# Two GNN layers over 32 batches: the last batch turned back to natural row order and stored by SyncE, two loads moved ahead, another order of the last additions

## The chip, the cores and the metric

The kernel runs on one core of one Trainium2 chip. The metric is the device time of one execution in microseconds; of several executions the median counts. In the profile PE is TensorE, PEld its weight loads, DVE VectorE, ACT ScalarE, POOL GpSimd and SP SyncE; a `q` behind a name means that engine's sequencer (waits, branches, DMA issues).

## The reference, cut to what matters

```python
# x: 32 x 512 x 512, adj: 512 x 512
h = relu(layernorm(x))                       # layer 0
x = x + einsum('nm,bmd->bnd', adj, h) @ W0 + b0
h = relu(layernorm(x))                       # layer 1: attention, 8 heads
q, k, v = h @ Wq + bq, h @ Wk + bk, h @ Wv + bv
scores = q k^T / 8 + (1 - adj) * -1e9        # per head
x = x + softmax(scores) v @ Wo + bo
```

The mask of layer 1 is so steep that each row's softmax has all its weight on the one column where adj is largest. The kernel tests this on the device at the start; it then computes layer 1 of row n as `h[argmax of adj in row n] @ (Wv Wo)` plus a constant row. Only the rows of h that some argmax names are needed, at most 336 of 512.

## The kernel before, in words

A batch is a 512 x 512 matrix of 1 MB, held as four chunks of 128 rows (chunk c is `X[b][:, c, :]`). From batch 5 on (`FIRST` is 4), the loop runs with the rows of a batch in another order, chosen so that much of `adj` is zero and layer 0 needs fewer products ("sparse", `spread`). `plan.xi` lists which natural row lies at which place: chunks are gathered from DRAM by it (`load_x`) and scattered back by it (`store_rows`, line 516, an indirect DMA on GpSimd). Where `back(b)` holds, a batch is first scattered into a DRAM buffer `xn` in natural order (`turn_back`, line 468), loaded again (`come_back`, line 478, four plain loads on SyncE), and then stored with plain DMAs (line 510). Before the change this is so for batches 29 and 30.

Iteration b of the loop has 21 steps. Each is a list of small pieces put there by `put(batch, step, f)`; a step's pieces are emitted just before the instruction that takes one result of TensorE out of PSUM. Steps 0 to 6 lie in layer 0 of batch b, 7 to 13 in the aggregation of batch b+1, 14 to 20 in layer 1 of batch b-1. So every engine's queue is in an order written out by hand, and an engine that waits holds up all that is behind it. `behind` makes each indirect DMA also wait for the PSUM result taken last before it in that order (`tick`), so that GpSimd keeps step with the rest.

The end is special. In iteration 31 (the last batch), steps 7 to 13 lie in layer 1 of batch 29 (TensorE from 968.87 us) and steps 14 to 20 in that of batch 30 (from 976.85 us). Layer 1 gives only the needed rows, z; they go to DRAM (`put_z`, line 773) and are fetched to the rows that want them (`fetch`, line 784, four gathers: `sel` for batch 29, `yT` for batch 30) and added (`add_z`, line 787), after which the chunk is stored. Layer 1 of batch 31 takes another way, to have no such round trip behind it: its h is stored as it is (`put_h`, line 683, two DMAs on SyncE), all 512 rows that the argmaxes name are gathered (`get_all`, line 495, four gathers `h<-hs`), and `layer1_rows` transposes chunk r (line 715), copies it (ScalarE, 716), multiplies it by `wvo` (727), adds it to x (730) and stores it, chunk by chunk. The additions and stores of batches 29 and 30 are placed between these chunks. Iteration 32 is only a list of pieces ahead of `layer1_rows`: the last z stores of batch 30, the transposes of chunk 0, `add_cvo` (719, a constant row added to x) and, before the change, `come_back(30)`.

`get_all` reads h by `plan.pq` (for rows in the loop's order); `plan.pi` is the same list for rows in natural order.

Behind the last instruction of this path stands a branch over the other path (line 980), and then the closing block (line 1658): SyncE waits for the semaphores of all DMAs, each engine reports (`DRAIN`), GpSimd collects the reports.

Of the kernel before, what the change touches and what calls it, by code (L numbers as in the profile page):

```python
# [408 lines left out]
def single_path(ctx: ExitStack, tc: tile.TileContext, x, adj, out, kept, room):  # L409
    nc = tc.nc  # L410
    B, N, D = x.shape
    C, DC = N // P, D // P
# [25 lines left out]
    hs_d = [dram.tile([N, D], F32, name=f"hs{i}") for i in range(3)]  # L438
# [5 lines left out]
    plan = Plan(tc, consts, dram, adj, kept, upper, B) if folded else None  # L444
# [5 lines left out]
    def phase(batches, sparse):  # L450
        with ExitStack() as inner:
            small = inner.enter_context(tc.tile_pool(name="small", bufs=4))
            ps_m = inner.enter_context(tc.tile_pool(name="ps_m", bufs=6, space=PSUM))
            ps_t = inner.enter_context(tc.tile_pool(name="ps_t", bufs=2, space=PSUM))
            run_phase(batches, sparse, small, ps_m, ps_t)

    def run_phase(batches, sparse, small, ps_m, ps_t):
        ordered = folded and (sparse or batches[0] == 0)

        def natural(b):  # L460
            return not ordered or b <= FIRST

        def back(b):
            return sparse and ordered and B - 3 <= b < B - 1

        def turn_back(b, chunks):
            for c in chunks:
# [20 lines left out]
        def behind(move):  # L488
            for taken in clock:
                tc.add_manual_dep(move.ins, taken.ins.name, mybir.DependencyInfo(  # L490
                    mybir.DependencyClass.Sync, mybir.DependencyReason.DATA), reason="in step")
            return move

        def gather(dst, rows, at, **more):
            return behind(nc.gpsimd.indirect_dma_start(out=dst, out_offset=None, in_=rows,  # L495
                                                       in_offset=bass.IndirectOffsetOnAxis(ap=at, axis=0), **more))
# [11 lines left out]
        def store_rows(b, c, eng):  # L508
            if natural(b) or back(b):
                stored = eng.dma_start(out[b, c * P:(c + 1) * P, :], X[b][:, c, :])  # L510
                if sparse:
                    for other_rows in stored_rows:
                        tc.declare_no_dep(stored.ins, other_rows.ins, reason="other rows")
                    direct_rows.append(stored)
                return
            stored = behind(nc.gpsimd.indirect_dma_start(  # L516
                out=out_rows, out_offset=bass.IndirectOffsetOnAxis(ap=plan.xi[:, b, c:c + 1], axis=0),
                in_=X[b][:, c, :], in_offset=None))
            nc.gpsimd.memset(gap, 0.0)
            for other_rows in stored_rows + direct_rows:  # L520
                tc.declare_no_dep(stored.ins, other_rows.ins, reason="other rows")
            stored_rows.append(stored)
# [87 lines left out]
        def places():  # L610
            table = dram.tile([N, 1], I32, name="table", bufs=1)
            nc.sync.dma_start(table.rearrange("(c p) o -> c (p o)", p=P), dest_r)
            return table

        def look_up(table, chunks):
            for c in chunks:
                gather(place[:, c:c + 1], table, idx[:, c, 0:1])
# [89 lines left out]

        def get_all(b, chunks=range(C)):
            for c in chunks:
                gather(hs[0][:, c, :], hs_d[b % 3], idx[:, c, 0:1] if natural(b) else plan.pq[:, c:c + 1])  # L710

        def transpose_all(r):
            pt = ps_t.tile([P, DC, P], F32, name="pt")
            for d in range(DC):
                nc.tensor.transpose(pt[:, d, :], hs[0][:, r, d * P:(d + 1) * P], ident)
            nc.scalar.copy(hs[1][:, :, r * P:(r + 1) * P], pt)
# [4 lines left out]
        def layer1_rows(b):  # L721
            for r in range(C):
                bank = ps_m.tile([P, D], F32, name="mm")
                for d in range(DC):
                    if d == 2 and r + 1 < C:
                        transpose_all(r + 1)
                    nc.tensor.matmul(bank, hs[1][:, d, r * P:(r + 1) * P], wvo[:, d, :], start=(d == 0),  # L727
                                     stop=(d == DC - 1))
                x_r = X[b][:, r, :].rearrange("p (q c e) -> p q c e", q=4, c=4)
                nc.vector.tensor_add(x_r, bank.rearrange("p (c q e) -> p q c e", q=4, c=4), x_r)  # L730
                store_rows(b, r, nc.sync)
                if sparse and r == 0:
                    for c in range(C):
                        add_z(B - 3, c, nc.sync)
                    fetch(B - 2)
                if sparse and r >= 2:
                    for c in ((0, 1, 2), (3,))[r - 2]:
                        add_z(B - 2, c, nc.scalar if c % 2 else nc.sync)
                for i in range(0 if sparse else 2):
                    add_z(B - 3 + r // 2, 2 * (r % 2) + i, nc.sync if r < 2 else nc.scalar)  # L740
# [34 lines left out]
        def place_of(b, c):  # L775
            return (place if natural(b) else plan.home if back(b) else plan.place)[:, c:c + 1]
# [5 lines left out]
        def fetch(b, chunks=range(C)):  # L782
            for c in chunks:
                gather(late_z[b][:, c, :], z_d[b % 3], place_of(b, c))

        def add_z(b, c, eng):
            nc.vector.tensor_add(X[b][:, c, :], late_z[b][:, c, :], X[b][:, c, :])
            store_rows(b, c, eng)
# [18 lines left out]
        for b in batches:  # L807
            todo = [[] for _ in range(21)]

            def put(batch, step, f, *args):  # L810
                if 0 <= batch < B:
                    todo[step].append(lambda: f(batch, *args))
# [78 lines left out]
            if b < B - 1:  # L891
                put(b, 20 if not several else 17, get_h)
            elif not sparse:
                put(b, 13, get_all)
                for c in range(C):
                    put(b, 15 + c, add_cvo, c)
            elif b == B - 1:
                for c in range(C):
                    put(b, 13, get_all, [c])
                    put(b - 1, 2 * c, turn_back, [c])  # L900
            if sparse and b == B - 2:
                for c in range(C):
                    put(b - 1, c, turn_back, [c])
                put(b - 1, 9, come_back)
# [37 lines left out]
            if sparse and b == B:  # L942
                put(b - 1, 1, lambda b: transpose_all(0))
                put(b - 2, 2, put_z, 6, S, range(2, 4))
                put(b - 2, 2, put_z, 0, 6, range(2, 4))
                put(b - 2, 2, come_back)
                for c in range(C):
                    put(b - 1, 1, add_cvo, c)
            if b == 1:
                tables = []  # L950
                put(1, 0, lambda b: tables.append(places()))
                for c in range(C):
                    put(1, 3 + c, lambda b, c: look_up(tables[0], [c]), c)
# [15 lines left out]
        if batches[-1] == B:  # L969
            layer1_rows(B - 1)  # L970
# [692 lines left out]
```

## Time and profile before

| | us |
|---|---|
| median of 3 runs (1020.17 to 1023.55) | 1021.16 |
| the profiled execution | 1016.16 |
| its span, first to last instruction | 1014.4 |
| PE busy | 988.0 (97%) |
| DVE busy | 801.9 (79%) |
| POOL busy | 591.1 (58%) |
| ACT busy | 586.1 (58%) |
| last TensorE matmul ends | 1001.57 |
| last engine instruction ends (POOL, line 519) | 1004.68 |

The profiled execution lies 5.0 us under the median of the runs, and 1.76 us of it lie outside its span. Sums below are made on the clock of the profile, in us from the start of the span. TensorE's granted clock is 0.992 of full over the span and 1.00 in the last 30 us until the matmuls end. Where a row of the timeline stands for several instructions, its second number is from the start of the first to the end of the last.

### The profile page before, as it was taken

How to read it: one execution, taken by the hardware profiler on the slowest of the kernel's cores; microseconds unless marked ns; L12 is line 12 of the kernel's file. 1: busy time of each engine (PE TensorE's matmuls, PEld its weight loads, DVE VectorE, ACT ScalarE, POOL GpSimd, SP SyncE). 2: the span in 40 equal slices, each digit the busy share in tenths (PEclk: the TensorE clock that was granted, in tenths of full speed). 3: DMA queues.
4: the chain of work that ended last, by engine and by line, in shares of the span. 5: the costliest groups of instructions: out<-in, count | busy, mean ns of one | idle time of the engine just before them, and what ended most of it. 6: DMA issues, size and time to landing. Idle time of an engine off the chain costs nothing.

```text
span 1014.4 us, 17265 instructions
## 1 busy us (share of the span) xinstructions
PE 988.0 (97%) x5627; PEld 886.9 (87%) x5627; DVE 801.9 (79%) x1792; ACT 586.1 (58%) x1282; POOL 591.1 (58%) x666
## 2 busy tenths in 40 slices
PE   7999999998999999999999999999999999999994
PEld 6468999897999999999999999999999999999882
DVE  4998897667888877778887777788877777888773
ACT  2765364556755555667655555676555556675330
POOL 1032366656666666666666666666766666667543
PEclk8999999999999999999999999999999999999998
DMA  9214558788888888888888888998888888888867
GB/s 312 82 65 152 113 164 250 220 223 219 207 226 206 201 221 209 231 221 207 211 194 207 219 207 227 225 223 202 201 203 213 209 219 227 221 209 207 210 209 265
DMA packets 161884, 208.90 MB, mean 206 GB/s; under 512 B 16556, under 2 KB 104376, under 8 KB 161784
## 3 DMA queue, kind: packets, MB, share of 16 engines
q0 software_dynamic: 44544, 120.10, 48.5%
q1 hardware_dynamic: 115480, 85.66, 29.2%
q10 hardware_dynamic: 1760, 1.93, 0.5%
q8 instruction: 46, 0.75, 0.3%
q14 instruction: 54, 0.44, 0.2%
HBM read 123.55 MB, written 84.09 MB: 205 GB/s over the span
## 4 chain that ended last, share of the span: by engine, by line
PE 72%; DMA 2%; POOL 2%; issue 2%; DVE 1%; ACT 1%; SPq 0%; POOLq 0%; ACTq 0%; DVEq 0%
PE mm L532 50%; PE mm L652 13%; PE mm L655 7%; PE mm L649 2%; DMA hc<-hs 1%; POOL x L495 1%; DMA pi<-posd,idx 1%; DMA z<-zr 1%; DMA hs<-h,dest 0%; POOL hs L692 0%; POOL out_dram L516 0%; POOL yT L495 0%; PE mm L727 0%; ACT h L379 0%; DVE st L361 0%
## 5 line engine op out<-in xcount | busy, mean ns | idle before, releaser
L588 DVE TENSOR_TENSOR x<-mm,x 128x512 f32<-128x512 f32 x217 | 148.8, 686 | 130.2 <-PE mm L532 128.2
L495 POOL DMA_INDIRECT x<-z,pplace x96 | 153.5, 1599 | 81.8 <-ACT yT L660 40.9
L379 ACT ACTIVATE h<-x,off,rstd 128x512 f32<-128x512 f32 x256 | 196.1, 804 | 7.3 <-DVE off L370 4.0
L532 PE MATMUL mm<-w_t,sel 128*128 128x256 f32 x744 | 171.7, 380 | 1.3 <-DVE x L588 1.3
L365 ACT ACTIVATE rstd<-mv,eps 128x2 f32<-128x2 f32 (+1 forms) x90 | 26.3, 292 | 241.8 <-DVE mv L362 241.8
L532 PEld LDWEIGHTS mm<-w_t,sel 128*128 128x128 f32 x744 | 140.6, 190 | 21.4 <-DVE x L588 2.5
L361 DVE BATCH_NORM_STATS2 st<-x 128x6 f32<-128x512 f32 x234 | 157.7, 674 | 1.1
L652 PE MATMUL mm<-ap,h 128*128 128x256 f32 x648 | 157.8, 380 | 0.0
L516 POOL DMA_INDIRECT out_dram<-x,xi x100 | 124.8, 1248 | 42.5 <-DVE zs L578 21.0
L495 POOL DMA_INDIRECT x<-in_x_dram,xi x108 | 104.0, 963 | 72.5 <-DVE x L588 37.4
L652 PEld LDWEIGHTS mm<-ap,h 128*128 128x128 f32 x648 | 114.9, 191 | 11.1
L495 POOL DMA_INDIRECT at<-in_x_dram,gi x81 | 76.9, 949 | 72.8 <-DVE st L361 25.0
L532 PE MATMUL mm<-w_s,yT 128*128 128x256 f32 x496 | 117.3, 379 | 0.8 <-ACT zs L580 0.8
L532 PE MATMUL mm<-hTs,wvo_t 128*128 128x168 f32 x720 | 113.4, 307 | 2.4 <-ACT zs L580 1.4
L532 PEld LDWEIGHTS mm<-hTs,wvo_t 128*128 128x128 f32 x720 | 105.4, 190 | 3.1 <-ACT zs L580 1.9
L580 ACT ACTIVATE zs<-mm,cvo_c 128x168 f32<-128x168 f32 x240 | 83.0, 398 | 38.2 <-PE mm L532 37.8
L532 PEld LDWEIGHTS mm<-w_s,yT 128*128 128x128 f32 x496 | 92.8, 190 | 12.3 <-ACT zs L580 1.0
L655 PEld LDWEIGHTS mm<-ag,adjT 128*128 128x128 f32 x648 | 89.3, 191 | 5.6
L655 PE MATMUL mm<-ag,adjT 128*128 128x128 f32 x648 | 89.7, 275 | 0.0
L627 DVE TENSOR_TENSOR x<-x,b_r 128x512 f32<-128x512 f32 x124 | 84.0, 678 | 0.0
L660 ACT COPY yT<-mm 128x512 f32<-128x512 f32 x108 | 61.5, 571 | 29.6 <-PE mm L655 29.6
L532 PE MATMUL mm<-hT,wvo 128*128 128x168 f32 x480 | 78.3, 306 | 0.0
(323 smaller groups left out, 1678.7 us busy)
## 6 DMA issues: line engine op xcount, KB each, us to landing
hc<-hs SPq DMA_DIRECT2D x124, 176.0 KB
z<-zr SPq DMA_DIRECT2D x120, 96.0 KB
hs<-h SPq DMA_DIRECT2D x52, 192.0 KB
z<-zr SPq DMA_DIRECT2D x120, 80.0 KB
hs<-h SPq DMA_DIRECT2D x52, 160.0 KB
out_dram<-x SPq DMA_DIRECT2D x26, 256.0 KB
x<-in_x_dram SPq DMA_DIRECT2D x12, 256.0 KB
x<-xn SPq DMA_DIRECT2D x8, 256.0 KB
```

Source lines behind the costliest of these rows:

```text
L361: self.nc.vector.bn_stats(st, self.src[:, self.chunks[i], :])
L365: self.nc.scalar.activation(self.rstd[:, 0:len(self.chunks)], self.mv[:, :, 1], AF.Sqrt, bias=self.eps)
L379: self.nc.scalar.activation(dst, src, AF.Relu, bias=self.off[:, i:i + 1], scale=self.rstd[:, i:i + 1])
L495: return behind(nc.gpsimd.indirect_dma_start(out=dst, out_offset=None, in_=rows, in_offset=bass.IndirectOffsetOnAxis(ap=at, axis=0), **more))
L516: stored = behind(nc.gpsimd.indirect_dma_start(out=out_rows, out_offset=bass.IndirectOffsetOnAxis(ap=plan.xi[:, b, c:c + 1], axis=0), in_= ...
L532: nc.tensor.matmul(bank[:, m, 0:half], lhs[:, k, m * P:(m + 1) * P], rhs[:, k, :], start=(first and m == 0 and k == 0), stop=(k == 1), ski ...
L580: taken = nc.scalar.activation(dst[:, m, :], bank[:, m, :], AF.Identity, bias=cvo_c[:, 2 * i + m:2 * i + m + 1])
L588: return nc.vector.tensor_add(dst, bank, dst)
L627: nc.vector.tensor_add(X[b][:, c, :], X[b][:, c, :], b0_r)
L652: nc.tensor.matmul(two(bank, j), H0[b][:, j, cols], two(plan.ap[:, j, :], j), start=False, stop=False, skip_group_check=True)
L655: nc.tensor.matmul(bank[:, j * P:(j + 1) * P], extra[:, j - 1, cols], plan.ag[:, j - 1, j * P:(j + 1) * P], start=False, stop=(j == C - 1) ...
L660: tick(nc.scalar.copy(yT[:, d, :], bank))
```

## The change

Batch 31 is turned back too: `back(b)` now holds for it. Its four chunks are scattered to `xn` at steps 7 to 10 of iteration 31, and loaded back at step 15. Its h is then gathered by `plan.pi`, its rows are added in natural order, and SyncE stores them with line 510 in place of GpSimd's line 516. `come_back(30)` moves from iteration 32 (behind the z stores) to step 9 of iteration 31, which on SyncE's queue is ahead of `put_h(31)`. `fetch(30)` moves from inside `layer1_rows` (behind the store of chunk 0) to the list ahead of it. VectorE's order in `layer1_rows` was: chunk 0, batch 29's four, chunk 1, chunk 2, batch 30's chunks 0, 1, 2, chunk 3, batch 30's chunk 3. It is now: chunk 0, batch 29's four, chunk 1, batch 30's chunk 0, chunk 2, batch 30's chunks 1, 2, 3, chunk 3.

```diff
         def back(b):
-            return sparse and ordered and B - 3 <= b < B - 1
+            return sparse and ordered and B - 3 <= b
...
-                gather(hs[0][:, c, :], hs_d[b % 3], idx[:, c, 0:1] if natural(b) else plan.pq[:, c:c + 1])
+                gather(hs[0][:, c, :], hs_d[b % 3], idx[:, c, 0:1] if natural(b) else plan.pi[:, c:c + 1])
...
                 if sparse and r == 0:
                     for c in range(C):
                         add_z(B - 3, c, nc.sync)
-                    fetch(B - 2)
-                if sparse and r >= 2:
-                    for c in ((0, 1, 2), (3,))[r - 2]:
+                if sparse and 0 < r < C - 1:
+                    for c in ((0,), (1, 2, 3))[r - 1]:
                         add_z(B - 2, c, nc.scalar if c % 2 else nc.sync)
...
                 for c in range(C):
                     put(b, 13, get_all, [c])
                     put(b - 1, 2 * c, turn_back, [c])
+                    put(b, 7 + c, turn_back, [c])
+                if sparse:
+                    put(b - 1, 9, come_back)
+                    put(b, 15, come_back)
...
                 put(b - 1, 1, lambda b: transpose_all(0))
                 put(b - 2, 2, put_z, 6, S, range(2, 4))
                 put(b - 2, 2, put_z, 0, 6, range(2, 4))
-                put(b - 2, 2, come_back)
                 for c in range(C):
                     put(b - 1, 1, add_cvo, c)
+                put(b - 2, 3, fetch)
```

## The prediction, on record before the changed kernel ran

> **What bounds the kernel now.** First the chain that ended last: up to 986 us it is nearly all TensorE, back to back, so nothing is won there; past it come GpSimd, waits and transfers. The change touches the trace from 963 us on, so I read that end by stage. Columns: stretch, its length, busy us of PE, PEld, DVE, ACT, POOL with counts, granted clock, busy share of the DMA engines, GB/s.
>
> ```profile
> 971.00:975.00 4.00, 4.00 (x31) 4.00 (x30) 3.52 (x12) 3.30 (x8) 0.00 (x0) 1.00 0.02 4
> 975.00:979.00 4.00, 4.00 (x31) 4.00 (x30) 3.86 (x8) 2.47 (x6) 0.00 (x0) 1.00 0.76 281
> 985.00:990.00 5.00, 4.18 (x16) 2.21 (x15) 4.13 (x6) 1.75 (x4) 3.29 (x5) 1.00 0.85 241
> 990.00:996.00 6.00, 6.00 (x19) 2.80 (x18) 2.67 (x4) 0.59 (x1) 3.96 (x6) 1.00 1.03 312
> 996.00:1002.00 6.00, 5.57 (x16) 2.35 (x14) 3.37 (x5) 0.59 (x1) 3.82 (x6) 1.00 1.05 412
> 1002.00:1006.50 4.50, 0.00 (x0) 0.00 (x0) 1.98 (x3) 0.00 (x0) 1.07 (x2) 0.78 1.06 400
> ```
>
> The DMA engines are empty from 971 to 975 and full from 990 to 1006.5, with 400 GB/s until 5 us after the last matmul. GpSimd has its hole in the same place. The timeline of GpSimd and VectorE (start, duration, engine, line; in brackets the idle time ahead):
>
> ```profile
> 969.30 0.17 POOL L762 MEMSET zs<- 128x64 f32 x1
> 980.10 1.00 POOL L495 DMA_INDIRECT h<-hs,pq  x1 [10.63 <-DVE adjT_s L347]
> ...
> 1002.64 0.68 DVE L730 TENSOR_TENSOR x<-mm,x 128x512 f32<-128x512 f32 x1
> 1003.61 0.96 POOL L516 DMA_INDIRECT out_dram<-x,xi  x1 [2.99 <-DVE x L730]
> 1003.91 0.69 DVE L787 TENSOR_TENSOR x<-yT,x 128x512 f32<-128x512 f32 x1 [0.58 <-DMA yT<-z,phome]
> 1004.57 0.11 POOL L519 MEMSET gap<- 128x1 f32 x1
> ```
>
> TensorE ends at 1001.57, but chunk 3 of batch 31 is added 1.07 us later, because batch 30's additions ahead of it wait for their gathers, whose transfers queue. Each DMA of this stretch lands 4.6 to 7.6 us after its issue, where z stores from 977.7 to 980.6 took 1.8 to 2.1 (landings are the trace's semaphore records). The last store is issued at 1004.63 and lands at 1009.21.
>
> Then the close, line 1658 (min/median/max in ns, first and last start):
>
> ```profile
> L1658 POOLq DRAIN  x3: 51/103/4592, 1008.7 to 1014.1; - x3
> ```
>
> GpSimd's first DRAIN runs from 1008.67 to 1013.26, and the other engines have reported by 1010.13 (SyncE, last). From 1013.26 to the end is 1.12. So 3.1 us of the end are GpSimd's alone.
>
> **The change, part by part.**
>
> *turn_back(31).* Four scatters on GpSimd. Its neighbours in the trace (L468) take 0.96 plus a memset of 0.11 and start every 1.28. x of batch 31 is complete at 970.38 (last L588), so they run from about 970.7 to 975.7. The hole is 10.6 us long, and the next GpSimd instruction starts at 980.1: nothing on GpSimd. If the hole were gone, they would cost 5.1 us.
>
> *come_back(30), moved.* Four loads on SyncE, 0.43 each (median of L478). They wait for the scatters of batch 30, the last of which landed at 971.01; so they are issued from 971.1 to 972.9. Behind them on SyncE is `put_h(31)`, ready at 974.70: 1.8 us of slack. In the tail the same 1.05 MB goes away (it was issued at 988.80 to 991.81): at 412 GB/s 2.5 us of a full queue.
>
> *come_back(31).* Four loads on SyncE behind the z stores of batch 29 (issued until 981.66), so 981.7 to 983.5; next on SyncE are z stores at 985.94. They need the turned rows, landed by about 978. Their user, `add_cvo`, ran at 986.70 to 989.20 and must only be done by 990.43. ScalarE's four z stores reuse the DMA semaphores of these loads, so they may wait until they land, near 987, up to 1 us later than before; behind them on ScalarE is the copy of chunk 1, 1.7 us later. I take nothing, at most 1 us.
>
> *The price: h of batch 31 comes later.* Between 972 and 979 the DMA engines moved 1.05 MB (h, landed 979.24). Now 3.15 MB want to pass there: the load of x30 and the scatters of batch 31, 2.1 MB, ahead of or beside h. The gap from 971.9 to 975.5 holds some 3.6 us of work: by the 383 GB/s that h itself reached at its best (977 to 978), 3.15 MB take 8.2 us and end at 980.1, which lands near 980.5; so h is 1.3 us late. With the rate of the same load of batch 29 alone (1.05 MB from 946 to 949.8, 275 GB/s) it would be 4.5 us late; with a perfect fit 0. The Trainium skill ("DMA: Bandwidth & Descriptors", Queues, rings and completion order) says that a DMA engine takes packets round-robin from the queues that have work: GpSimd's scatters then take half while h goes out, which speaks against the change. The same page (Specifications) puts the limit of HBM per core at 358 GB/s; by it they take 8.8 us and h is 1.9 us late. The rows above show 400 to 412 over 10 us in this traffic, above the rule, so I stay with 1.3.
>
> The first h gather then starts at 981.4. Chunk 0 landed 4.0 us after its issue (984.11), 0.6 us before TensorE wanted it (984.69). Beside the loads of x31 I add 0.4: 985.8, so TensorE stands still for 1.1 us (0 to 2.5 with the bounds 0 and 2.7 for h; 6 at the worst rate). Chunks 1 to 3 had 2.3, 5.6 and 7.6 us of slack. TensorE ends at 1002.7. GpSimd's zero fill of z (L762, behind the gathers) and the z transposes and stores of batch 30 shift by the same 1.3.
>
> *fetch(30) and the stores of batch 31.* The gathers `yT` lay behind one L516 (0.99 + 0.12) and began at 993.21, when the z stores, landed by 992.33, had let them. Now they follow the `sel` gathers at once: shifted by 1.3, z lands about 992, since 1 MB less runs beside it, so the gathers start at 992.4 to 996.2. Their time to land was 6.3 to 6.9; with x30's 1.05 MB gone (2.5 us of queue) I take 5, so the last is there at 1001.2 (4 to 6.9: 1000.2 to 1003.1). VectorE's last `add_z` of batch 30 ends by 1002.0, before TensorE is through. So the new order, which puts all four additions of batch 30 ahead of chunk 3, costs 0; if the gathers land as slowly as before, 1.1. Four scatters leave GpSimd (1.1 each) for four stores of 0.33 on SyncE, which otherwise waits there.
>
> *The close.* Chunk 3 is added from 1002.7 to 1003.4, and SyncE issues its store at 1003.5; by the 2.75 of the fastest plain 0.26 MB transfer here (L478) it lands at about 1006.3. SyncE branches 0.39 after issuing (1002.75 to 1003.14 before): 1003.9. Then it got its next instruction only after 3.94 us, and the one behind that after 2.29 more, though the semaphores they name had been complete for long. The skill ("Runtime: NRT & Kernel Launch", Instruction fetch mechanics) says that a taken branch to a far target forces a fetch of its page, while running on over a page boundary is mostly hidden. The trace agrees on the first (8 KB packets of the instruction queue from 1005.3 on) and not on the second: the 2.29 stood open. Whether a boundary falls there again depends on the length of the program, so I take half, 1.15 (0 by the rule, 2.29 by the row); and 3.1 for the first fetch, between 2.29 on idle DMA engines and 3.94 on full ones. The remaining waits take 0.76 (1009.37 to 1010.13), the closing 1.12. Sum: 1003.9 + 3.1 + 1.15 + 0.76 + 1.12 = 1010.0.
>
> GpSimd's last instruction ends near 997.2 rather than 1004.68. With the fetch as long as it had been (5.29 from branch to DRAIN) and the DRAIN at 4.59 it reports at 1007.1, ahead of SyncE at 1008.9: its 3.1 us vanish beneath SyncE.
>
> The span goes from 1014.4 to 1010.0, 4.4 us less: 3.1 of it GpSimd's end, the rest the shorter fetch, with TensorE's 1.1 of delay against the 1.07 that VectorE was late. The profiled execution would be 1011.8; the same off the median gives 1016.8.
>
> **Rivals.**
>
> *A, forecast:* 1016.8, from 1014.5 (TensorE not delayed, no second fetch) to 1019 (second fetch as before, TensorE 2 us late). Chance 0.68, of which 0.56 gains over 3.06 us.
>
> *B, GpSimd's DRAIN is not hidden:* the trace has one such DRAIN behind DMAs, and it began within 0.05 us of the landing of GpSimd's last store (1008.71). If it measures something that ends after all transfers, it runs from 1006.3 to 1010.9, and the end is 1012.0: 2.4 less, 1018.8. The same comes out if TensorE stands 3 us. For it: one sample. Against it: GpSimd's transfers are done 5 us before the others. Chance 0.21.
>
> *C, h comes too late:* the loads of x30 and x31 crowd out h's stores and gathers. At 275 GB/s the store is late by 4.5, and the gathers share with x31's load, 1.05 MB, 2 us more: TensorE stands 6 us from 984.7, ends at 1007.6, and the end is 1014.9, with slow fetches 1018: 1021.7 to 1025. It decides from a stall of 5.5 us on. For it: that row; chunk 0's 0.6 us of slack. Against it: the row is a load alone, with engines idle between its packets (share 0.85), and mixed traffic reaches 400. Chance 0.11, 0.07 of it over 3 us slower.
>
> That the tail's queue stays full is no case of its own: without x30 some 5.7 MB pass from 989 on, at 350 GB/s until 1005.3, which is where TensorE's end puts the last store as well.
>
> **Numbers.** A measurement tells about 0.3% (3.06 us). Faster 0.56, from A; within 0.3%: 0.12 of A, B, and 0.04 of C, 0.37; slower 0.07. The range leaves out C and A's best edge: 1014.4 to 1021.2.
>
> **What would show it.** Right: the DMA share between 971 and 975 near 1; TensorE's wait ahead of the first L715 near 1.1 us; L730's last row within 0.1 us of TensorE's end; transfers landing in 3 to 5 us after 996; GpSimd's DRAIN over before SyncE's last wait. Wrong: h gathers starting after 984; a gap ahead of L715 over 3 us; a DRAIN that still ends 3 us behind SyncE; VectorE waiting for `yT` after 1002.7.

## The result, and the profile after

| | before | after |
|---|---|---|
| median of 22 runs each, same chip, us | 1021.57 | 1021.52 |
| ratio after to before, 95% interval | | 1.0000 (0.9986 to 1.0014) |
| the profiled execution, us | 1016.16 | 1025.84 |
| its span, us | 1014.4 | 1024.0 |

The forecast was 1016.8, 4.4 us of gain. Nothing was gained: the interval allows 1.4 us either way.

The two spans must not be subtracted. Of their 9.6 us, 5.4 are there before the last batch begins, in work that both kernels have alike. So all that follows is counted from one event: TensorE's first product of layer 0 of batch 31 (956.03 us in before, 961.42 in after). Times on this clock are called *tail times*, and the time from there to the end of the span is the *tail*. Before has a tail of 58.4 us, and of 58.3 in a second trace. The changed kernel was profiled three times: 62.6, 59.9 and 62.3. One execution scatters by some 2 to 3 us there, so what counts below is the order of events, which is the same in all three, and the timed ratios.

The stages of after. The columns are stretch, length, busy us of PE, PEld, DVE, ACT, POOL with counts, granted clock, DMA share, GB/s. Each row but the last starts 5.39 us later than its counterpart of before.

```profile
976.39:980.39 4.00, 3.83 (x26) 3.32 (x25) 2.99 (x11) 2.94 (x9) 3.23 (x6) 1.00 0.59 170
980.39:984.39 4.00, 2.89 (x21) 2.63 (x20) 2.88 (x6) 1.79 (x3) 1.08 (x2) 1.00 1.04 403
990.39:995.39 5.00, 2.07 (x15) 1.81 (x13) 1.71 (x4) 0.69 (x2) 3.93 (x6) 1.00 0.96 299
995.39:1001.39 6.00, 5.11 (x12) 2.57 (x13) 3.29 (x6) 0.59 (x1) 3.24 (x4) 0.55 0.94 299
1001.39:1007.39 6.00, 6.00 (x18) 2.94 (x17) 3.09 (x5) 1.17 (x2) 1.49 (x2) 0.88 0.61 208
1007.39:1011.89 4.50, 4.50 (x15) 2.22 (x14) 1.45 (x3) 0.59 (x1) 2.54 (x3) 1.00 0.92 272
1011.89:1016.39 4.50, 3.33 (x8) 1.14 (x6) 2.01 (x3) 0.00 (x0) 0.00 (x0) 1.00 0.79 295
```

The empty stretch is filled (4 GB/s before, 170 now) and the one behind it is full (403). Then come two things that before does not have: in the third row TensorE is busy for only 2.07 of 5 us, and in the fourth it runs at a granted clock of 0.55. The full queue of before (1.03 to 1.06 from 990 on) has become a queue with room in it (0.61 in the fifth row), and TensorE still works where it had been done. GpSimd, VectorE and the row of TensorE's stall, from the timelines of after:

```profile
980.54 0.96 POOL L468 DMA_INDIRECT xn<-x,xi  x1 [0.19 <-issue]
989.65 0.98 POOL L495 DMA_INDIRECT h<-hs,pi  x1 [8.04 <-DVE h0s L578]
995.61 0.78 PE L715 MATMUL pt<-ident,h 128*128 128x128 f32 x4 [3.15 <-DMA h<-hs,pi]
997.06 3.78 PE L727 MATMUL mm<-wvo,h 128*128 128x512 f32 x4 [0.68 <-ACT h L716]
1005.60 1.19 POOL L495 DMA_INDIRECT yT<-z,phome  x1 [6.06 <-DMA z<-hc]
1017.17 0.69 DVE L786 TENSOR_TENSOR x<-yT,x 128x512 f32<-128x512 f32 x1 [0.92 <-DMA yT<-z,phome]
1017.78 0.68 DVE L730 TENSOR_TENSOR x<-mm,x 128x512 f32<-128x512 f32 x1
```

The scatters of batch 31 end at 981.5 and GpSimd is idle for 8.0 us more: the hole held them, as forecast. But the first gather of h starts at 989.65, tail time 28.2 in place of 24.1; TensorE stands 3.15 us for it, and its next four products take 3.78 us. In before the same place reads:

```profile
984.83 0.60 PE L715 MATMUL pt<-ident,h 128*128 128x128 f32 x4
986.25 1.98 PE L727 MATMUL mm<-wvo,h 128*128 128x512 f32 x4 [0.82 <-ACT h L716]
```

No stall, and 1.98 us for the same four. The close of after, line 1661 (it was 1658; min/median/max in ns, first and last start):

```profile
L1661 POOLq DRAIN  x3: 51/103/8637, 1010.9 to 1023.7; - x3
L1661 SPq DRAIN  x3: 7/7/7, 1022.8 to 1023.1; - x3
```

GpSimd's long DRAIN now runs from 1010.89 to 1019.53 and is over 3.3 us ahead of SyncE's report at 1022.8. That gain is there. The chain that ended last shows what took its place (start, us, what):

```profile
982.20 6.66 DMA hs<-h
...
1001.70 3.08 DMA z<-hc
...
1009.59 7.56 DMA yT<-z,phome
```

The second store of h takes 6.66 us (3.13 in before), and behind it the round trip of z ends the kernel.

### The profile page after: what moved, and what is told of

Its sections match the earlier page's. It is cut to its first block, busy times and chain, and to the rows that moved or that the text cites. A ratio compares the mean times of both kernels' runs of the same rounds, so it can differ in the third digit from the quotient of the medians.

```text
span 1024.0 us, 17279 instructions
## 1 busy us (share of the span) xinstructions
PE 993.7 (97%) x5627; PEld 889.3 (87%) x5627; DVE 801.4 (78%) x1792; ACT 585.8 (57%) x1282; POOL 590.9 (58%) x666
## 4 chain that ended last, share of the span: by engine, by line
PE 88%; DMA 3%; DVE 3%; issue 2%; ACT 1%; SPq 0%; another core or an unknown queue 0%; POOL 0%; ACTq 0%; POOLq 0%; DVEq 0%
PE mm L532 60%; PE mm L652 13%; PE mm L655 7%; PE mm L649 2%; PE mm L271 1%; PE mm L673 1%; PE mm L150 1%; DMA x<-in_L_gnn_Wv_dram 1%; DMA ap<-in_adj_dram,xi 1%; DMA yT<-z,phome 1%; DMA hs<-h 1%; ACT h L379 1%; DVE x L588 0%; DVE st L361 0%
## 5 line engine op out<-in xcount | busy, mean ns | idle before, releaser
L495 POOL DMA_INDIRECT x<-z,pplace x96 | 153.5, 1599 | 81.7 <-ACT yT L660 40.9
L532 PEld LDWEIGHTS mm<-w_t,sel 128*128 128x128 f32 x744 | 140.8, 190 | 23.7 <-DVE x L588 4.2
L516 POOL DMA_INDIRECT out_dram<-x,xi x96 | 120.5, 1255 | 39.2 <-DVE zs L578 20.1
L532 PEld LDWEIGHTS mm<-w_s,yT 128*128 128x128 f32 x496 | 93.7, 192 | 15.1 <-ACT zs L580 3.5
```

What stands on the lines that cost most here:

```text
L516: stored = behind(nc.gpsimd.indirect_dma_start(out=out_rows, out_offset=bass.IndirectOffsetOnAxis(ap=plan.xi[:, b, c:c + 1], axis=0), in_= ...
L532: nc.tensor.matmul(bank[:, m, 0:half], lhs[:, k, m * P:(m + 1) * P], rhs[:, k, :], start=(first and m == 0 and k == 0), stop=(k == 1), ski ...
```

## The experiments

In what follows x30 and x31 are the x of batches 30 and 31, z30 is the z of batch 30, and h is that of batch 31. There are three theories.

*Theory 1, crowding:* x30's load and the scatters of batch 31 hold up the stores of h; TensorE stands for h, its clock falls, and this costs as much as the close gains. *Theory 2, a shared semaphore:* the program has eight semaphores for the plain DMAs and hands them out in turn, in the order in which the schedule expects the DMAs. With eight loads added ahead of them, SyncE's first store of z30 gets the semaphore of ScalarE's first, and has to wait until that has landed. From the timeline of after:

```profile
996.64 1.89 ACTq L772 DMA_DIRECT2D z<-hc  x4
1000.34 1.84 SPq L772 DMA_DIRECT2D z<-hc  x4
```

In before both engines issued these stores from 985.94 on. *Theory 3, traffic:* the turned-back batch adds 2.1 MB (a scatter and a load) to a tail that had 13.6 MB in the packet records of before and has 15.7 in after (packets of instructions left out), so something may have to end later wherever they are put.

Edits are of the changed kernel unless said otherwise. Every ratio is against before on the same chip. "h" is the start of the first gather of h, "stall" TensorE's wait ahead of the first L715, "PE" TensorE's end, "yT" the first gather of z30, all in tail time.

| run | h | stall | PE | yT | tail | ratio (95% interval) |
|---|---|---|---|---|---|---|
| before | 24.1 | 0 | 45.5 | 37.2 | 58.4 | |
| before2 | 24.1 | 0 | 46.5 | 38.5 | 58.3 | one trace |
| after | 28.2 | 3.2 | 53.8 | 44.2 | 62.6 | 1.0000 (0.9986 to 1.0014) |
| after2 | 27.7 | 4.6 | 52.8 | 43.4 | 59.9 | 1.0013 (1.0003 to 1.0022) |
| after3 | 27.7 | 3.9 | 53.8 | 43.5 | 62.3 | 1.0000 (0.9983 to 1.0016) |
| x30_behind_h | 25.4 | 0.5 | 46.1 | 43.5 | 61.2 | 1.0034 (1.0020 to 1.0047) |
| turn31_alone | 25.4 | 0.9 | 47.1 | 41.7 | 59.4 | 1.0002 (0.9990 to 1.0013) |
| z30_sync | 28.2 | 4.5 | 52.5 | 43.4 | 60.5 | 1.0022 (1.0012 to 1.0032) |
| a_x31act | 27.7 | 0 | 51.2 | 41.8 | 58.6 | 0.9989 (0.9972 to 1.0005) |
| b_x31act_x30late | 24.8 | 0.6 | 47.8 | 39.8 | 57.3 | 0.9984 (0.9966 to 1.0001) |
| c_x31act_x30_15 | 25.8 | 0.4 | 48.1 | 42.6 | 58.4 | 1.0000 (0.9984 to 1.0016) |
| x30_alone | 24.5 | 0 | 51.4 | 43.3 | 62.1 | 1.0019 (1.0003 to 1.0035) |
| order_alone | 23.7 | 0 | 46.1 | 39.1 | 58.6 | 0.9999 (0.9980 to 1.0018) |
| keep_clock | 27.6 | 1.3 | 58.0 | 43.7 | 64.1 | 1.0047 (1.0030 to 1.0064) |
| keep_clock2 | 27.6 | 0 | 55.3 | 43.9 | 61.5 | 1.0031 (1.0017 to 1.0044) |
| g_both_late | 25.2 | 0 | 52.3 | 38.2 | 60.1 | 1.0008 (0.9991 to 1.0024) |
| i_z30sync_x30late | 25.2 | 0 | 47.5 | 41.0 | 58.1 | 1.0003 (0.9987 to 1.0018) |
| h_x31act20_x30late | 25.0 | 0 | 47.4 | 40.9 | 58.3 | 0.9993 (0.9977 to 1.0010) |

**after2 and after3**, the changed kernel again, beside two of the groups below.

> The changed kernel once more, to see how far one profile of its end stands for it. Measure in all runs: the tail, from TensorE's first product of batch 31's layer 0 to the end of the span. It was 58.4 us in the profile of before and 62.6 in that of after, though the medians agree within 0.05 us. Theory 1 (crowding): the load of x30 and the scatters of batch 31 stand ahead of and beside the two stores of h, whose second landed 3.1 us after its issue before and 6.9 after; the gathers of h, TensorE's start of the last batch and all behind it come later by that, and TensorE, having stood still for 3 us, runs its next products at half the granted clock. Then the stall ahead of the first L715 is there again, 2 to 4 us, with a granted clock under 0.8 behind it. If that stall was an accident of one execution, it is under 1 us and the tail is near 54 to 58.

> The changed kernel once more, beside the next three on one chip: tail 60 to 62.6 us, TensorE standing 3 to 5 us ahead of the first transpose of h, ratio 0.9995 to 1.002.

Both show the late h, the stall and the late yT. In after and after3 the interval holds 1; in after2 it lies above it, 0.03 to 0.22% slower. In none is a gain over 0.17% left open.

**x30_behind_h**: the loads of x30 behind h.

```diff
-                    put(b - 1, 9, come_back)
+                    put(b - 1, 15, come_back)
```

> The changed kernel with the load of x30 put behind the stores of h and of batch 29's z (step 15, ahead of the load of x31). Theory 1 (crowding): half of what stands ahead of h is gone; the second store of h lands within 4.5 us of its issue, TensorE stands at most 1 us ahead of the first L715 and keeps its clock, and the tail is 3 to 5 us shorter than that of the changed kernel: faster by 0.3 to 0.5%. Theory 2 (shared semaphore): in the changed kernel SyncE's first z store of batch 30 has the DMA semaphore of ScalarE's first one and is issued only when that has landed, 3.7 us later; that wait is still in this kernel, so the gathers of batch 30's z stay as late against their z as before, and the tail changes by under 1 us. The two loads together, 2.1 MB, now run beside the gathers of h: if these take over 6 us to land, the gain is lost to them.

**turn31_alone**: the loads of x30 in their old place, behind the z stores; only batch 31's own part is left ahead.

```diff
-                    put(b - 1, 9, come_back)
...
+                put(b - 2, 2, come_back)
```

> The changed kernel with the load of x30 left in its old place behind the z stores. Theory 1: the scatters alone stand beside h (1.05 of 2.1 MB), so h's second store lands about 4.5 us after its issue, the stall is near 1 us, and the load of x30 is back in the full end: tail near 58, time within 0.2% of both kernels. Theory 2: in this kernel no z store of SyncE has the semaphore of one of ScalarE's, so the gathers of batch 30's z start 3 to 4 us sooner behind their z and the tail is 3 to 4 us shorter than in the changed kernel.

Both take most of the stall away, as theory 1 has it. From the waits of TensorE in turn31_alone (engine, line, what for: us in total, times, longest):

```profile
PE pt L715 <- DMA h<-hs,pi: 1.3, 2, 0.9
```

With the scatters alone h is 1.3 us late, with x30's load on top 3.6. But the end does not come earlier. In both, SyncE issues its z stores 6 us behind ScalarE's (31.2), at 37.7 in x30_behind_h and at 37.2 in turn31_alone, although their data are there. In turn31_alone SyncE's first z store has the semaphore of ScalarE's first, which landed at 37.1: theory 2's crossing, which I had not seen when I wrote what I expected of this run. In x30_behind_h the first load of x31, ahead of the z stores on SyncE, has it and goes out only when ScalarE's store has landed, at 35.7; VectorE then waits 7.65 us for x31, until 39.7. The two causes had to be taken apart differently.

**z30_sync**: all eight z stores of batch 30 on SyncE, so no semaphore is shared between engines.

```diff
-                eng = nc.scalar if q > 1 and b == B - 2 else nc.sync
+                eng = nc.sync
```

> The changed kernel with all eight z stores of batch 30 issued by SyncE (ScalarE issues none), which takes the shared semaphore away and costs SyncE four issues of 0.45 us. Theory 2: z of batch 30 lands some 2 us sooner (3.7 less 1.8), its gathers start sooner by that, and the end with it: tail 2 us shorter, 0.2%. Theory 1: h is as late as in the changed kernel, TensorE stands 2 to 4 us and runs at the lower clock behind it; the end is TensorE's, so the tail is less than 1 us shorter.

Nothing is gained: one engine needs from 34.0 to 38.2 to issue all eight, the gathers yT start when they did, and TensorE ends as late.

**a_x31act, b_x31act_x30late, c_x31act_x30_15**: ScalarE loads x31, which puts the semaphores in another order; x30 is at step 9 (a), behind the z stores (b) or at step 15 (c).

```diff
-                load = nc.sync.dma_start(X[b][:, c, :], xn_d[b % 3][c * P:(c + 1) * P, :])
+                load = (nc.scalar if b == B - 1 else nc.sync).dma_start(X[b][:, c, :], xn_d[b % 3][c * P:(c + 1) * P, :])
```

> The changed kernel, but the four loads of x31 are issued by ScalarE in place of SyncE, so that no z store of SyncE shares a DMA semaphore with one of ScalarE. Theory 1 (h of batch 31 is crowded: gathers of h start 3.6 us later, TensorE stands 4.6 us and is slow after it): the stall stays at 4 to 5 us, TensorE ends at 52 to 53 us of the tail, the z stores of batch 30 go out at 35 on both engines and the gathers yT start 2.5 to 3.5 us earlier (about 40.5), but nothing gains by it: tail 59 to 60 us, ratio 1.000 to 1.0015. Theory 2 (the shared semaphore, which holds SyncE's z stores for 3.5 us, sets the end): tail 56 to 57 us, ratio about 0.997.

> As the run before it, with the loads of x30 back in their old place behind the z stores of batch 30. Both causes together: gathers of h start at 25.4 us of the tail (1.3 late, from the scatters of batch 31 alone), TensorE stands under 1 us and ends at 46 to 47, the z stores of batch 30 go out at 31 to 33 on both engines, the gathers yT start at 37 to 38.5 and land in 6 us beside x30: last addition near 47, tail 54 to 55.5 us, ratio 0.995 to 0.997. If the semaphore is worth nothing: the tail of the version with x30 behind h, 61 us, ratio 1.003. If the crowding is worth nothing beyond what the shared semaphore does: the same tail as with x30 ahead of h and x31 on ScalarE.

> The changed kernel with the loads of x31 on ScalarE and those of x30 on SyncE at step 15 (behind h, ahead of the z stores of batch 30). Both causes together: gathers of h near 25.4 us of the tail, stall of TensorE under 1.5 us, its end at 46 to 47.5, gathers yT from 37 to 38.5 and landing in 5 us, since the load of x30 is over by then: tail 53 to 55 us, ratio 0.994 to 0.996. If loads at step 15 crowd the gathers of h as those at step 9 crowd h's stores: a stall of 3 us or more and a tail over 57.

In a, both engines issue the z stores from 35.1, and yT starts 1.6 us earlier than in after2, half of what I expected; TensorE's delay sits elsewhere (it waits 2.3 us inside its products for ScalarE, whose queue is held by the loads of x31 until the scatters have landed), and its end is late all the same. Behind that wait its clock is at 0.50 for 3.41 us; the wait and the stage behind it:

```profile
989.66 2.37 PE L532 MATMUL mm<-adjT_s,wvo_t 128*128 128x168 f32 x8 [2.29 <-ACT h0s L580]
990.43:992.43 2.00, 2.00 (x9) 2.00 (x9) 0.30 (x1) 0.00 (x0) 1.46 (x2) 0.50 1.01 314
```

The tail, 58.6, is below theory 1's 59 to 60 and far from theory 2's 56 to 57: theory 2 alone does not set the end. b, with most of the stall and the crossing between the z stores taken away, has the best ratio of all. Its gain of 1.6 us (interval 3.5 to -0.1) falls short of the 3 to 5 expected. c misses: its third z store on SyncE is issued only at 37.2, because its semaphore had gone to ScalarE's first z store: in this order the semaphores are crossed again.

**before2**, a second trace of before.

> The kernel before once more, for a second trace of its end: a tail within 0.7 us of 58.4 us, no stall of TensorE ahead of the first product by wvo, gathers of h at 24 us of the tail and GpSimd's DRAIN as the last to end, 4 to 5 us long.

It came out so, but for yT, 1.3 us later.

**x30_alone and order_alone**: the kernel before with one part of the change each.

```diff
+                if sparse:
+                    put(b - 1, 9, come_back)
...
-                put(b - 2, 2, come_back)
```

```diff
-                    fetch(B - 2)
-                if sparse and r >= 2:
-                    for c in ((0, 1, 2), (3,))[r - 2]:
+                if sparse and 0 < r < C - 1:
+                    for c in ((0,), (1, 2, 3))[r - 1]:
...
+                put(b - 2, 3, fetch)
```

> The kernel before with one part of the change: the loads of x30 at step 9 of iteration 31, ahead of h; batch 31 is not turned back and VectorE's order is the old one. If those 1.05 MB ahead of h cost what they cost on top of the scatters of batch 31 (2.3 us): gathers of h start at 25.5 to 26.5 us of the tail (24.06 before), TensorE stands 1.5 to 2.5 us, and 1.05 MB less runs in the tail, so that the gathers yT land in under 6 us; GpSimd's DRAIN still ends last: tail 58 to 60 us, ratio 0.9995 to 1.0015. If the load fits into the empty 3.6 us ahead of h as predicted: gathers of h within 0.3 us of 24.06, no stall, tail 57 us, ratio 0.998.

> The kernel before with one part of the change: the gathers yT follow the sel gathers at once, and VectorE takes all of batch 30 ahead of chunk 3 of batch 31; nothing is loaded or scattered earlier. No stall of TensorE. Gathers yT start 0 to 1 us earlier, the additions no earlier than they land; the last scatter of GpSimd and its DRAIN of 4.6 us still close the kernel: tail 57.5 to 58.7 us, ratio 0.999 to 1.0005. If the order itself did harm, chunk 3 would wait for yT and the tail would be 60 or more.

The new order is worth nothing by itself. The early load of x30 by itself hardly moves h (24.5): alone it does fit into the empty stretch. Its tail is long for a reason that neither theory had (see the last section), and the ratio says 0.03 to 0.35% slower.

**keep_clock and keep_clock2**: TensorE is given work in its stall, to hold its clock: 22 transposes of the identity, or ten products of 512 columns. The edit of keep_clock2:

```diff
+            for i in range(10 if sparse and r == 0 else 0):
+                nc.tensor.matmul(pt.rearrange("p d n -> p (d n)"), ident, wvo[:, 0, :], start=(i == 0), stop=(i == 9))
             for d in range(DC):
```

> The changed kernel with 22 transposes of the identity ahead of the first transpose of h, into the PSUM tile that the real ones then overwrite: TensorE works through the time in which it stood for h. If the slow first row after the stall is the clock that falls in it: granted clock 1.00 throughout, row 0 takes 3.9 us in place of 5.0 to 5.4, TensorE ends at 50 to 50.8 us of the tail in place of 52.8. The tail gains less than that, since the additions of batch 30 ahead of chunk 3 end at 53 us whatever TensorE does: tail 59 to 59.8 us, ratio 1.0 to 1.001. If the row is slow for another reason (loads that share memory with it), TensorE's end stays at 52.5 or later.

> The changed kernel with ten plain products of 512 columns (4.3 us, one accumulation, so one semaphore increment) ahead of the first transpose of h, in place of the 22 transposes tried before. Those kept the clock at 1.00 up to h, but then ScalarE got TensorE's signal 4.5 us late and all was lost. If the many increments had been the cause of that: the copy of chunk 0 follows the transposes within 0.2 us, the clock stays at 1.00, row 0 takes 3.9 us, TensorE ends 2 us earlier than in the changed kernel, tail 59 to 60 us, ratio 0 to 0.001 under the changed kernel's. If work in TensorE's stall does harm in itself: tail over 62 and a ratio 0.002 or more above the changed kernel's.

The first failed: the copy of chunk 0 came 4.5 us behind the transposes. In the second I had the duration wrong (each product shows in the trace as two passes of 0.43 us, so the ten filled 8.6 us and h had to wait for them), but it measures what was wanted. The stages from the end of layer 1's last products on, after3 first:

```profile
984.33:988.33 4.00, 0.29 (x3) 0.04 (x1) 1.36 (x2) 0.69 (x2) 3.01 (x4) 1.00 0.92 281
988.33:990.33 2.00, 1.18 (x5) 0.85 (x6) 2.00 (x4) 0.58 (x1) 1.67 (x2) 0.64 0.99 374
990.33:992.33 2.00, 2.00 (x3) 0.74 (x3) 0.72 (x2) 0.00 (x0) 1.28 (x2) 0.50 0.91 275
```

and keep_clock2:

```profile
987.18:991.18 4.00, 4.00 (x12) 1.88 (x11) 1.42 (x2) 0.69 (x2) 3.05 (x5) 1.00 1.00 359
991.18:993.18 2.00, 2.00 (x6) 0.95 (x5) 2.00 (x5) 0.00 (x0) 1.70 (x2) 1.00 0.84 251
993.18:995.18 2.00, 2.00 (x6) 0.87 (x5) 0.66 (x2) 0.00 (x0) 1.23 (x2) 1.00 1.04 315
```

TensorE idles in the first and its clock is halved; in the second it is busy and stays at 1.00. From the first transpose of h to TensorE's end it then takes 16.6 us in keep_clock2 (38.74 to 55.34) against 19.6 in after3 (34.15 to 53.76) and 16.7 in before. So the stall costs 3.0 us once more through the clock. The ten products put the first transpose of h off by 4.6 us against after3, which fits that the whole is slower all the same; a version with five was not run.

**g_both_late**: neither load ahead of the z stores; x31 on ScalarE, x30 on SyncE, both at step 2 of iteration 32. In this order x31 is loaded behind the addition of the constant row, so that row is missing from batch 31.

> Batch 31 turned back and stored by SyncE as in the change, but neither load ahead of the z stores of batch 30: x31 by ScalarE and x30 by SyncE, both behind them. Only the scatters of batch 31 stand beside h, nothing holds ScalarE, and no z store shares a semaphore with the other queue's. Gathers of h at 24.8 to 25.5 us of the tail, stall under 1 us, z stores at 30 to 31.5, yT from 36.5 to 38 on, VectorE's first addition waits for x31 until 39 to 40, TensorE ends at 46 to 47, additions of batch 30 over by 47 to 49: tail 53.5 to 56 us, ratio 0.995 to 0.998. If 2.1 MB of loads beside the z round trip cost as much as the early loads did: yT later than 39.5, tail over 57, ratio 0.9985 or more.

h and yT came as expected, but x31 is late, and that holds two engines. VectorE waits 7.8 us for it ahead of the first L730 (until 42.9). ScalarE, whose queue issues its loads from 34.1 to 38.5, copies chunk 1 late; TensorE waits 2.75 us for this copy, and its clock is at 0.50 for the 3.41 us behind that.

**i_z30sync_x30late and h_x31act20_x30late**: b's idea by other means. i has the z stores on SyncE as in z30_sync and x30 behind them; h has x31 on ScalarE at step 20 and x30 behind.

> The changed kernel with all eight z stores of batch 30 on SyncE and the loads of x30 behind them; x31 as in the change. No crossed semaphore, ScalarE is held by no load and no store, and only the scatters of batch 31 and x31's load stand beside h and its gathers. Gathers of h at 25 to 25.5 us of the tail, stall under 1 us, TensorE ends at 46 to 47.5, z stores from 30 to 34, yT from 38 to 39.5, additions of batch 30 over by 48.5 to 50: tail 54.5 to 57 us, ratio 0.996 to 0.9985, under the changed kernel's by 0.002 or more. If only the early load of x30 mattered and the rest is chance: tail over 58.5.

> As the version with x31 on ScalarE and x30 behind the z stores (tail 57.3 us), but ScalarE issues the loads of x31 at step 20 in place of 15, behind its last sums, where their wait for the scatters holds nothing up. TensorE's end 1 to 1.5 us earlier (46 to 47 us of the tail), x31 lands by 37: tail 55.5 to 57 us, ratio 0.9965 to 0.9985. If x31 lands too late for row 0's addition, VectorE and then TensorE wait: tail over 58.5.

In both TensorE is hardly harmed (its end at 47.5 and 47.4, 2.0 us later than in before) and the clock stays at 1.00, and still neither is faster than before. The stages of i, and VectorE's first addition of batch 30:

```profile
985.26:993.26 8.00, 6.46 (x32) 4.42 (x31) 4.75 (x8) 1.75 (x4) 4.96 (x7) 1.00 1.00 325
993.26:1001.26 8.00, 8.00 (x26) 3.92 (x25) 4.55 (x7) 1.17 (x2) 3.16 (x4) 1.00 1.05 373
1001.26:1009.26 8.00, 3.49 (x9) 1.23 (x7) 3.50 (x6) 0.00 (x0) 1.39 (x2) 0.99 0.97 365
```

```profile
1004.45 0.69 DVE L786 TENSOR_TENSOR x<-yT,x 128x512 f32<-128x512 f32 x1 [3.37 <-DMA yT<-z,phome]
```

The DMA engines are full in all three stages, and VectorE waits 3.37 us for the first gather of z and about 0.5 for each of the next two. From tail time 28 to the last data packet the engines move 344 GB/s in i, 335 in b, and 262 to 272 in the three traces of the changed kernel, where TensorE ends 5 to 6 us later. The last data packet ends at 52.7 in before, at 54.4 in b and 54.8 in i.

This is what theory 3 would look like, but that the bytes set the end is not shown: no run takes them away and leaves the rest. In the runs b, h and i the round trip of z starts late and is not slower. The last store of z30 is issued at 33.9 in b, 35.3 in h and 36.0 in i (31.3 in before, 32.2 in before2). From there the first gather of yT follows after 5.9, 5.7 and 5.0 us (5.8 and 6.3), and its addition 5.4 to 6.9 us behind that (6.5 in before). The traces show nearer reasons for the late stores: the gathers of h still start 0.7 to 1.1 us late; SyncE waits for the semaphores of earlier DMAs, in run h until 33.46 for one of x31's loads, in b for z stores of batch 29; and in i one engine issues all eight, from 31.05 to 35.98. In i the parts add up as follows: TensorE ends 2.0 us later than in before, chunk 3 is added 4.3 us behind it (1.1 in before), and from there to the end it takes 6.35 (11.8), so that 58.1 stands against 58.4.

## Why the prediction was wrong

The forecast was a span 4.4 us shorter; the tail of after2 is 1.5 us longer, and its ratio of 1.0013 is 1.3 us. The sum taken apart (us against before; the trace of before has TensorE's end 12.9 ahead of the end of the span):

| term | predicted | after2 | after | after3 |
|---|---|---|---|---|
| h's first gather later | 1.3 | 3.6 | 4.2 | 3.6 |
| TensorE's end later | 1.1 | 7.2 | 8.3 | 8.2 |
| VectorE's chunk 3 behind TensorE's end (1.1 before) | 0 | 0.85 | 2.6 | 2.3 |
| from chunk 3's addition to the end | 7.3 | 6.25 | 6.24 | 6.26 |

**What failed is the step "the price: h of batch 31 comes later".** The mechanism was named and its size was not: 1.3 us of lateness and 1.1 of standing became 3.6 and 7.2 to 8.3. In after2, whose records are the most complete, it goes as follows. The packets of the scatters, of x30 and of h are 3.15 MB, as I had counted. Megabytes by microsecond of tail time:

| from | 16 | 17 | 18 | 19 | 20 | 21 | 22 | 23 | 24 | 25 | 26 |
|---|---|---|---|---|---|---|---|---|---|---|---|
| before, loads and stores of x and h | 0 | 0 | 0 | 0.16 | 0.35 | 0.38 | 0.16 | 0 | 0 | 0 | 0 |
| after2, scatters | 0 | 0.21 | 0.05 | 0.19 | 0.16 | 0.15 | 0.16 | 0.11 | 0.02 | 0 | 0 |
| after2, loads and stores of x and h | 0.06 | 0.21 | 0.34 | 0.22 | 0.22 | 0.22 | 0.27 | 0.29 | 0.24 | 0.03 | 0.01 |

From 17 to 25 that is 3.05 MB in 8 us, 381 GB/s: my rate of 383 was right, the 275 of rival C was not, and 381 is above the 358 GB/s that the Trainium skill ("DMA: Bandwidth & Descriptors", Specifications) gives as the limit of HBM for one core. Two other things were missing. But for 0.05 MB, the traffic begins at 16.9 and not at 15.9, though the first scatter and load were issued at 14.6 and 15.1: 1.0 us. And a transfer has landed when its last packet has: 0.04 MB straggle between 25 and 27, so the store lands at 26.9 in place of the 24.5 that an even fit gives with the start as I had it, 1.4 us beyond the late start. My 1.3, this 1.0 and these 1.4 make 3.7; the store landed 3.65 us later than in before, and the gather behind it started 3.6 later. The round robin that the prediction quotes from the Trainium skill ("DMA: Bandwidth & Descriptors", Queues, rings and completion order) spoke for a late last packet: while h goes out, scatters take 0.11 to 0.19 of each 0.37 to 0.43 MB, a quarter to nearly a half. I had this rule before me and took an average rate for a last packet. Not in the table, and not in my sum, are 0.56 MB of batch 29's z stores, which run between 24 and 27; whether they hold up the last packets of h was not tried.

The rest follows from it. Chunk 0 lands 5.85 us after its gather's issue (4.0 + 0.4 expected), beside x31's load; that is 27.66 + 5.85 = 33.5, against 28.96, when TensorE was through: a stall of 4.6. The bounds I gave ended at 2.5, with 6 only for the slowest rate.

**The clock was not in the sum at all.** From the first transpose of h to TensorE's end, 16.7 us became 19.2 (after2) and 19.6 (after, after3), and keep_clock2 gave the 3.0 back. In all three traces the granted clock goes to 0.50 some 3.5 to 4.3 us after the last product ahead of the stall, and stays there for 6.83 us. The Trainium skill ("TensorE: Matmul & The Clock Gate", HAM oscillation — how this bites in real kernels) warns of idle gaps of over about 3.4 us between matmuls. Shorter ones were enough here: in after the clock fell 0.39 us into the transposes that ended the wait of 3.15 us, and waits of 2.29 us (a_x31act) and 2.75 us (g_both_late) halved it too, while waits of up to 1.74 us (before2) left it at 1.00. My range for the stall went up to 2.5 us and, in rival C, to 6; from about 2.3 on it should have carried that price.

**The gather of z and VectorE's order.** I expected yT at 36.4 in tail time and it came at 43.4 to 44.2. Most of this comes from h. GpSimd's zero fill of z (L761, it was L762) lies behind the gathers of h, as the prediction says, and VectorE's transposes of z follow the zero fill. In before, and then in after:

```profile
985.07 1.71 DVE L768 STREAM_TRANSPOSE hc<-h0s 128x640 f32<-128x640 f32 x2 [0.60 <-POOL h0s L762]
```

```profile
994.40 0.17 POOL L761 MEMSET h0s<- 128x64 f32 x1
994.60 1.70 DVE L767 STREAM_TRANSPOSE hc<-h0s 128x640 f32<-128x640 f32 x2 [2.66 <-issue]
```

The second view names no releaser, but VectorE starts 0.03 us after the zero fill ends. In tail time the transposes start at 29.0 in before, at 33.2 in after and at 32.6 in after2, where I had shifted them by 1.3. ScalarE's z stores, behind its copy of chunk 0, start at 34.9 to 35.2 in the three traces (29.9 in before). The crossed semaphore, which I had looked for at x31's loads and not between the two z stores, holds SyncE's for 3.4 to 3.9 us more. In a_x31act, without the crossing, yT is 1.6 us and the tail 1.2 us earlier than in after2 (on another chip). The sentence that the new order "costs 0; if the gathers land as slowly as before, 1.1" named the right place and not the right condition: in after2 the gathers yT land in 5.8 to 6.0 us, faster than the 6.3 to 6.9 of before, but they start 6.2 to 7.0 us later. So chunk 3, placed behind batch 30's additions, is added 0.85 to 2.6 us behind TensorE's end in the three traces.

**What was right.** The scatters ran in GpSimd's hole and cost nothing there. The DRAIN of GpSimd is hidden in every version with the SyncE store but keep_clock (there it starts at 63.35 and is 0.25 us long, SyncE having reported at 62.77): rival B is false. The close is even shorter than expected, 6.25 us from chunk 3's addition against 7.3, because SyncE waited 3.17 us for its first instruction behind the branch (3.1 expected) and not at all for the second (half of 2.29 expected): this fits the rule that the prediction quotes from the Trainium skill ("Runtime: NRT & Kernel Launch", Instruction fetch mechanics), that running on over a page boundary is mostly hidden, and my half was wrong.

**Where the gain went.** The close gives back 12.9 - 0.85 - 6.25 = 5.8 us in after2, and TensorE's end takes 7.2. Rival C described this ("h comes too late", decided "from a stall of 5.5 us on"), but it needed the slow rate; the stall was 3 to 5 us, and the clock made up the rest. And the variants show that it is no accident of one placement: in the runs b, h and i the stall is at most 0.6 us, and yT still starts at 39.8 to 41.0 (37.2 and 38.5 in the two traces of before), because the last store of z30 goes out late. That the 2.1 MB set the end there, the full queue that I had dismissed as "no case of its own", is argued and not shown. What stays is 0 to 0.34% for the best, b, with an interval that just reaches 1; no version was shown to be faster than before.

Open is why the traffic starts a microsecond late when loads and scatters come together, and how much of the scatter between after2 and after is chance.

## What to carry to other kernels

A transfer moved into an empty stretch costs nothing only if its last packet, not its mean rate, is through before the next user; count from the first packet, and put a stall's aftermath (the clock) into the sum from about 2.3 us of standing on. Where a change adds bytes to a tail whose DMA engines are full, ask what will be late in each place where they can be put, before choosing the place. And where DMAs of two engines draw semaphores from one rotation, adding loads ahead can make one engine's store wait for another's.

## What the runs showed of the hardware

TensorE's signal can be late. In keep_clock the last transpose of h ends at 990.06, and ScalarE's copy of its result, with nothing else to wait for, starts 4.5 us later:

```profile
989.40 0.66 PE L717 MATMUL pt<-ident,h 128*128 128x128 f32 x4 [1.28 <-DMA h<-hs,pi]
994.58 0.58 ACT L718 COPY h<-pt 128x512 f32<-128x512 f32 x1 [8.05 <-remote]
```

TensorE's semaphore shows its increments of this time at 33.4, 36.3 and 39.1 to 39.2 in tail time, the last three together, where the transposes ended at 34.7. In x30_alone it is the same, once: the increments come 2.7 and 3.7 us late, and TensorE then stands 4.4 us for ScalarE. Smaller delays are in all other traces but five. In nine (after, after3, a, b, g, h, i, keep_clock and keep_clock2) VectorE's sums near tail time 20 start 0.5 to 1.7 us behind their products, and TensorE then waits 1.0 to 1.2 us for VectorE near 21; after2 has no such wait. Elsewhere the delays are up to about 1 us. The five traces without any are before, after2, x30_behind_h, turn31_alone and z30_sync. No such delay was found for VectorE's or ScalarE's semaphores.

What causes it is not settled. keep_clock2, with fewer increments and the DMA engines as full, shows none at its copy, which speaks for many increments in a short time, but x30_alone had only two. Four of the five traces without delays are all that were taken on one chip, and the five are also the only ones in whose records no increment of TensorE is missing. So the chip, or the recording of the trace itself, is not ruled out.

The half clock comes in steps of 3.41 us. It lasts 3.41 us behind the waits of 2.29 (a_x31act) and 2.75 us (g_both_late), 6.83 behind waits of 3.15 to 4.6 us (the three traces of the changed kernel, z30_sync and x30_alone), and 10.24 behind one of 5.16 us (keep_clock). So its price grew with the stall, but not evenly: between 3.15 and 4.6 us it was the same.
